# The biases of a graph network's products folded into a row of ones, and a maximum in place of a Relu

## The chip, the cores and the metric

The kernel runs on one core of a Trainium2 chip. The core has five engines that run their own instruction queues and wait for each other by semaphores: TensorE (PE, matrix products into PSUM), VectorE (DVE, element by element work), ScalarE (ACT, functions, copies, scale and bias), GpSimd (POOL, element by element work[...]) and SyncE (SP, which here only issues DMA transfers). The metric is device microseconds of one execution, from which the median of several runs is taken.

## The reference, cut to what matters

There are 64 graphs of 256 nodes with 256 channels. Layer 0 normalizes the adjacency matrix by its degrees, mixes the nodes with it, applies a linear map with bias `b0`, adds the residual and takes a layer norm. Its result is `x1`, so each node's channels of `x1` sum to zero. Layer 1 works on `x1`:

```
h      = relu(bn1(conv1 x1))                        # 1x1 convolution: a product over channels
x_conv = relu(bn2(conv2 h) + x1)                    # 17 taps along the nodes
s      = x1 w_se^T + b_se;  A = exp(-|s_n - s_m|^2) # 3 columns
x_nmp  = A relu(x1 w_msg^T + b_msg)
gi     = [x_conv, x_nmp] w_ih^T + b_ih;   gh = x1 w_hh^T + b_hh      # three blocks r, z, n
r, z   = sigmoid(gi_r + gh_r), sigmoid(gi_z + gh_z)
new    = (1 - z) tanh(gi_n + r gh_n) + z x1
out    = layernorm(x1 + new)
```

All of it is fp32.

## The kernel before, in words

The work goes graph by graph, in 4 groups of Q = 16 graphs. `layer0(g)` makes `x1`, stores it in `x1_d` and leaves it in SBUF. `x1_transposed(g)` transposes it on PE and copies it with ScalarE (L429) into `xn[:, :2]`, the channels on the partitions. `layer1(g)` then forms, in this order: `h` (conv1, with the three columns of `w_se` beside it, 259 columns; VectorE adds the bias row `bc1` for each half of the nodes, L446, and ScalarE takes the Relu of both halves, L447); the columns of `s` for the distances (L451 to L456, `scols`); `msg` (VectorE adds `bmsg_t`, L467, ScalarE takes the Relu, L468); the transform of `h` along the nodes (`p_dft`, L480); the distances and `A` (`p_rows`, `p_dist`, `aT`); and `x_nmp` (`p_nmp`, L513). The transposed `x1` and `x_nmp` go to DRAM as `xn_d[g]`.

conv2 is done for 16 graphs at once in a frequency domain: products with the transformed taps (`p_k`, L539), and the transform back, a long series of VectorE instructions on the tile `VM` (L588 to L747), which ends with stores to `xc_d`.

The gates of a graph are `gru(g)`. `load_gate` and `load_conv` fetch `x1`, `xn_d` and `xc_d`; `transposed(g)` brings x_conv into `inputs` (where `in_blocks` is true, for the first 4 graphs of each group and all 16 of the last, 28 in all, by a VectorE transpose in blocks, L805, an addition of the transposed `x1` on GpSimd, L806, and two Relus on ScalarE, L808; for the other 36 by PE transposes, L814, and two Relus, L816). `input_sums` forms four sums on GpSimd (L825 to L830). The r and z products use a Winograd form of seven block products of 128 by 256 with the weights `wrz`: 42 matrix instructions a graph (L846) into the four PSUM banks `p15`, `p26`, `p7`, `p34`. VectorE adds the bias `brz_t` while it moves `p15` out (`first`, L859), then forms the other sums (L860 to L869). The n products are 24 instructions (L883) into `p_n`, whose left half holds gi_n and right half gh_n, with `bn_t` added to both (L888), then L889, L892 and a tanh (L895), and the layer norm of the result (L906 to L910 with `layernorm`, L320 to L333). `p15`, `p26`, `p7`, `p34` and `p_n` share a pool of four banks (`psacc`), so the first `p_n` of a graph takes the bank of `p15` when L859 has read it.

Three things set the order of the instructions. Generators are advanced in a written order (`graphs`, `gates`, `merge`). In the stretches run by `paced`, each instruction passed to `mark` lets some pieces of the transform back be traced, and `tc.issue_after` queues those of its instructions that are on the marked instruction's engine behind it. And the compiler's list scheduler, which runs a model of the engines, fixes the order within each engine's queue: among the instructions that are ready in its model the earlier traced one goes first.

Of the kernel before, what the change touches and what calls it, by code (L numbers as in the profile page):

```python
# [9 lines left out]
F32 = mybir.dt.float32  # L10
# [4 lines left out]
P = 128  # L15
# [11 lines left out]
def kernel(  # L27
# [87 lines left out]
    wc1 = const.tile([P, DCH, D + NSE], F32)  # L115
    bc1 = const.tile([P, D + NSE], F32)
    wmsg = const.tile([P, DCH, D], F32)
    bmsg_t = const.tile([P, D], F32)
    alpha_t = const.tile([P, 1], F32)
# [6 lines left out]

    nc.scalar.copy(bc1[:, :4], neg_half)
    for i, a in enumerate((bn1_g, bn2_g, bn1_b, bn2_b, bn1_m, bn2_m, bn1_v, bn2_v)):
# [5 lines left out]
    nc.sync.dma_start(wc1[:, :, D:], w_seT.rearrange("(k p) o -> p k o", p=P))  # L134
    nc.sync.dma_start(bc1[:, D:], bcast_rows(b_se, NSE))


    ident = const.tile([P, P], F32)
    make_identity(nc, ident)
    nc.vector.tensor_scalar(alpha_t, alpha_t, MIN_ALPHA, None, op0=ALU.max)  # L140

# [11 lines left out]
    wn = const.tile([P, 3 * DCH, D], F32)  # L153
    brz_t = const.tile([P, 2, D], F32)
    bn_t = const.tile([P, 2, D], F32)

    bn2_bias = const.tile([P, DCH], F32)

    def batch_norms(pool):


        scale = pool.tile([P, D], F32, name="scale")
        p = bank("p_bn")
        nc.tensor.transpose(p[:, :16], vectors, ident[:16, :16])
        cols = pool.tile([P, 4, 4], F32, name="bn")
        nc.vector.tensor_copy(cols.rearrange("p i n -> p (i n)"), p[:, :16])
        g, b, m, v = (cols[:, i, :] for i in range(4))
        nc.vector.tensor_scalar(v, v, BN_EPS, None, op0=ALU.add)
        nc.gpsimd.tensor_tensor(v, v, neg_half, op=ALU.pow)
        nc.vector.tensor_mul(g, g, v)  # L170
        nc.vector.tensor_mul(m, m, g)
        nc.vector.tensor_sub(b, b, m)
        nc.vector.tensor_copy(bn2_bias, b[:, 2:4])

        ones = pool.tile([P, P], F32, name="ones")
        nc.vector.memset(ones, 1.0)
        rows = [bank("p_norm") for _ in range(2)]
        for i, col in enumerate((g[:, 0:1], g[:, 1:2], b[:, 0:1], b[:, 1:2], g[:, 2:3], g[:, 3:4])):
            diagonal = pool.tile([P, P], F32, name="diagonal", bufs=2)
            nc.vector.tensor_scalar(diagonal, ident, col, None, op0=ALU.mult)  # L180
            nc.tensor.matmul(rows[i // 4][:, i % 4 * P : (i % 4 + 1) * P], ones, diagonal, start=True, stop=True)
        nc.scalar.activation(scale, rows[1][:, :D], AF.Copy, scale=2.0 / FL)
        nc.vector.tensor_mul(
            wc1[:, :, :D], wc1[:, :, :D], rows[0][:, :D].unsqueeze(1).to_broadcast([P, DCH, D])
        )
        nc.vector.tensor_copy(bc1[:, :D], rows[0][:, D:])
        yield scale
# [234 lines left out]
    def x1_transposed(g):  # L422
        x1 = X1.pop(g)
        xn = XN[g] = work.tile([P, 2 * DCH, N], F32, name="xn")
        p = bank("p_x1T").rearrange("p (k n) -> p k n", k=DCH)
        for k in range(DCH):
            for c in range(NCH):
                nc.tensor.transpose(p[:, k, c * P : (c + 1) * P], x1[:, c, k * P : (k + 1) * P], ident)
        nc.scalar.copy(xn[:, :DCH], p)  # L429

    def layer1(g, place):
# [6 lines left out]

        h = work.tile([P, NCH, D + NSE], F32, name="h", bufs=1)
        for c in range(NCH):  # L440
            p = bank("p_conv1")[:, : D + NSE]
            for k in range(DCH):
                nc.tensor.matmul(  # L443
                    p, x1T[:, k, c * P : (c + 1) * P], wc1[:, k, :], start=k == 0, stop=k == DCH - 1
                )
            mark(nc.vector.tensor_tensor(h[:, c, :], p, bc1, op=ALU.add))  # L446
        nc.scalar.activation(h[:, :, :D], h[:, :, :D], AF.Relu)  # L447

        s3 = h[:, :, D:]
        cols = scols.rearrange("p c (q r) -> p c q r", r=32)  # L450
        nc.vector.tensor_copy(cols[:, :, :, :NSE], s3.unsqueeze(2).to_broadcast([P, NCH, 4, NSE]))  # L451
        sq3 = small.tile([P, NCH, NSE], F32, name="sq3")
# [9 lines left out]
        for c in range(NCH):  # L462
            for k in range(DCH):
                nc.tensor.matmul(  # L464
                    p[:, c, :], x1T[:, k, c * P : (c + 1) * P], wmsg[:, k, :], start=k == 0, stop=k == DCH - 1
                )
        mark(nc.vector.tensor_tensor(msg, p, bmsg_t.unsqueeze(1).to_broadcast([P, NCH, D]), op=ALU.add))  # L467
        nc.scalar.activation(msg, msg, AF.Relu)  # L468
        yield
# [288 lines left out]

    GATE, CONV, SUMS = {}, {}, {}

# [21 lines left out]
    def load_gate(g):  # L782
# [3 lines left out]
        nc.sync.dma_start(inputs[:, : 2 * DCH], xn_d[g])  # L786
        GATE[g] = x1, inputs

    def sent(g):
# [10 lines left out]
    def transposed(g):  # L800
# [3 lines left out]
        if in_blocks(g):  # L804
            behind(nc.vector.transpose(xcT.rearrange("p k (s r) -> p k s r", r=RB), CONV.pop(g)))  # L805
            nc.gpsimd.tensor_tensor(xcT, xcT, inputs[:, :DCH], op=ALU.add)  # L806
            for k in range(DCH):
                nc.scalar.activation(xcT[:, k], xcT[:, k], AF.Relu, bias=bn2_bias[:, k : k + 1])  # L808
            return
# [22 lines left out]
    def gru(g):  # L832
# [25 lines left out]
        first = gate.tile([P, 2, D], F32, name="first", tag="gn")  # L858
        mark(nc.vector.tensor_add(first, half(p15), brz_t), 1)  # L859
        nc.vector.tensor_add(trz[:, 0:2], first[:, 0:1].to_broadcast([P, 2, D]), half(p26))  # L860
# [13 lines left out]
        for c in range(NCH):  # L874
# [6 lines left out]
            for o, part in ((1, terms[:DCH]), (0, terms[DCH:])):  # L881
# [5 lines left out]
            gn = gate.tile([P, 2, D], F32, name="gn")  # L887
            mark(nc.vector.tensor_add(gn, p.rearrange("p (i d) -> p i d", i=2), bn_t), 1)  # L888
            nc.vector.scalar_tensor_tensor(  # L889
                gn[:, 1, :], trz[:, 2 * c], 1.0, gn[:, 1, :], op0=ALU.add, op1=ALU.mult  # L890
            )
# [81 lines left out]
    with tc.tile_pool(name="setup", bufs=1) as setup:  # L973
        load_taps(setup, 0)
        nc.sync.dma_start(wmsg, w_msgT.rearrange("(k p) o -> p k o", p=P))
        nc.sync.dma_start(bmsg_t, bcast_rows(b_msg, D))
        firsts = merge(layer0(0), layer0(1))
# [6 lines left out]
        def gate_weights():  # L984
# [8 lines left out]
            for k, w in ((0, w_hhT), (DCH, w_ihT[D:]), (2 * DCH, w_ihT[:D])):  # L993
                nc.sync.dma_start(wn[:, k : k + DCH], w[:, 2 * D :].rearrange("(k p) o -> p k o", p=P))
            yield

# [6 lines left out]
        others = [weights(setup, i, scale2) for i in range(NPARTS)]  # L1003
        others += [take(more_weights, i) for i in (1, 2, 2)]
        run(graphs(0, range(Q), others))
        bih_t = setup.tile([P, 3 * D], F32, name="bih", tag="taps", bufs=2)
        nc.sync.dma_start(bih_t, bcast_rows(b_ih, 3 * D))
        bhh_t = setup.tile([P, 3 * D], F32, name="bhh", tag="taps", bufs=2)
        nc.sync.dma_start(bhh_t, bcast_rows(b_hh, 3 * D))
        brz = brz_t.rearrange("p i d -> p (i d)")  # L1010
        nc.vector.tensor_add(brz, bih_t[:, : 2 * D], bhh_t[:, : 2 * D])
        nc.vector.tensor_sub(brz_t[:, 1], brz_t[:, 1], brz_t[:, 0])
        nc.vector.tensor_copy(bn_t[:, 0, :], bih_t[:, 2 * D :])
        nc.vector.tensor_copy(bn_t[:, 1, :], bhh_t[:, 2 * D :])
    ustream = ctx.enter_context(tc.tile_pool(name="ustream", bufs=6))
# [142 lines left out]
```

## Time and profile before

| | us |
|---|---|
| median of 3 runs | 2145.82 |
| lowest and highest run | 2143.14, 2146.74 |
| span of the profiled execution | 2152.3 |
| busy in it: PE, DVE, ACT, POOL | 2052.7, 1581.6, 841.9, 664.8 |

The profile is of one execution. Its span, from the first to the last instruction, is 2152.3 us, and what lies around the span is not shown, so that execution took at least 2152.3 us, which is 6.5 us (0.3%) above the median of the runs. A profile line such as `L888 DVE TENSOR_TENSOR gn<-p_n,bn_t 128x512 ... x128 | 87.3, 682 | 17.8` names the line of the code, the engine, the operation, output and inputs, the shape and the count, then the busy time in us and the mean duration of one in ns, then the idle time of the engine just ahead of these instructions, and what ended it.

### The profile page before, as it was taken

To read this page: it belongs to the slowest core of one execution; us is meant where nothing else is said; L and a number is where in the kernel's file an instruction comes from. 1 tells how busy PE (TensorE), PEld (TensorE's weight loads), DVE (VectorE), ACT (ScalarE), POOL (GpSimd) and SP (SyncE) were. 2 spreads that over 40 slices of the span, in tenths; PEclk is the share of its full clock that TensorE was granted. 3 is DMA by queue.
4 is the path that set the end of the run, shared out by engine and by line. 5 is a ranking of instruction groups with operands and counts; after the bars stand their busy time and mean duration, and the time that the engine had idled before them with its cause. 6 is when DMAs were issued, how large, how long until landed. Compare 5 with 4: busy or idle time off the path is not lost.

```text
span 2152.3 us, 28977 instructions
## 1 busy us (share of the span) xinstructions
PE 2052.7 (95%) x9693; PEld 1735.8 (81%) x9693; DVE 1581.6 (73%) x3719; ACT 841.9 (39%) x1857; POOL 664.8 (31%) x640
## 2 busy tenths in 40 slices
PE   7999999887999999899999999999999998999997
PEld 5888788776888888788888888777888887788886
DVE  5555578775568788775656988876566889988887
ACT  4665643456431123445552122446553112222222
POOL 2444310121431244213322133323231123444442
PEclk9999999999999999999999999999999999999999
DMA  4766666434346644233326654324324744443331
GB/s 122 235 196 197 198 194 207 142 132 134 96 146 203 203 110 128 93 112 113 113 94 190 205 157 113 118 98 133 102 88 136 243 116 122 119 102 99 94 84 54
DMA packets 295085, 298.30 MB, mean 139 GB/s; under 512 B 76414, under 2 KB 273618, under 8 KB 294938
## 3 DMA queue, kind: packets, MB, share of 16 engines
q1 hardware_dynamic: 235050, 200.46, 30.9%
q10 hardware_dynamic: 44480, 67.39, 8.8%
q0 software_dynamic: 15408, 28.61, 6.1%
q8 instruction: 77, 1.26, 0.2%
q14 instruction: 70, 0.57, 0.1%
HBM read 193.28 MB, written 103.06 MB: 138 GB/s over the span
## 4 chain that ended last, share of the span: by engine, by line
PE 44%; DVE 12%; issue 9%; POOL 6%; ACT 4%; DMA 2%; ACTq 0%; SPq 0%; POOLq 0%; DVEq 0%
PE p_rz L846 14%; PE p_n L883 8%; PE p_k L539 7%; PE p_out L409 2%; PE p_nmp L513 2%; PE p_hT L399 2%; PE p_dft L480 2%; POOL ln_rs L323 2%; PE p_conv L443 1%; PE p_msg L464 1%; PE p_dist L504 1%; POOL sums L826 1%; POOL sums L825 1%; DMA u<-ud 1%; POOL xc_g L796 1%
## 5 line engine op out<-in xcount | busy, mean ns | idle before, releaser
L883 PE MATMUL p_n<-wn,inputs 128*128 128x256 f32 x1536 | 355.1, 385 | 13.4 <-DVE first L859 13.2
L846 PE MATMUL p_rz<-wrz,sums 128*128 128x256 f32 x1536 | 348.6, 380 | 1.3 <-DVE gn L888 0.8
L883 PEld LDWEIGHTS p_n<-wn,inputs 128*128 128x128 f32 x1536 | 288.5, 192 | 64.2 <-DVE first L859 20.9
L846 PEld LDWEIGHTS p_rz<-wrz,sums 128*128 128x128 f32 x1536 | 290.0, 190 | 44.5 <-issue 5.2
L846 PE MATMUL p_rz<-wrz,inputs 128*128 128x256 f32 x1152 | 271.6, 379 | 1.0 <-ACT inputs L808 1.0
L323 POOL TENSOR_TENSOR ln_rs<-ln_rs,neg_half 128x2 f32<-128x2 f32 x129 | 99.1, 768 | 510.9 <-DVE ln_rs L322 464.0
L846 PEld LDWEIGHTS p_rz<-wrz,inputs 128*128 128x128 f32 x1152 | 217.6, 190 | 31.1 <-ACT inputs L808 1.2
L895 ACT ACTIVATE nn<-gn 128x256 f32<-128x256 f32 x128 | 53.3, 417 | 332.1 <-DVE gn L892 331.7
L539 PE MATMUL p_k<-u,VM 128*128 128x256 f32 x736 | 175.2, 380 | 2.7 <-DMA u<-ud 1.9
L369 POOL TENSOR_TENSOR dis<-deg,neg_half 128x2 f32<-128x2 f32 x64 | 46.1, 720 | 423.6 <-DVE deg L367 393.1
L333 ACT ACTIVATE x_g<-x_g,ln_mr,ln_rs 128x256 f32<-128x256 f32 x128 | 70.0, 593 | 241.5 <-DVE ln_mr L331 241.5
L539 PEld LDWEIGHTS p_k<-u,VM 128*128 128x128 f32 x736 | 138.1, 190 | 24.4 <-DMA u<-ud 4.1
L480 PE MATMUL p_dft<-fwd,h 128*128 128x240 f32 x512 | 120.2, 379 | 25.9 <-ACT h L447 24.6
L399 PE MATMUL p_hT<-adjT,x 128*128 128x256 f32 x512 | 129.8, 397 | 14.0 <-DVE adjT L381 7.6
L825 POOL TENSOR_TENSOR sums<-inputs 128x384 f32<-128x384 f32 x64 | 67.1, 1048 | 239.0 <-ACT inputs L816 206.3
L480 PEld LDWEIGHTS p_dft<-fwd,h 128*128 128x128 f32 x512 | 95.2, 192 | 47.6 <-ACT h L447 41.2
L506 DVE TENSOR_TENSOR aT<-aT,adjT 128x512 f32<-128x512 f32 x64 | 44.6, 698 | 118.2 <-ACT aT L505 118.1
L443 PE MATMUL p_conv<-wc,xn 128*128 128x259 f32 x512 | 125.8, 388 | 4.3 <-ACT xn L429 4.3
L392 POOL TENSOR_TENSOR x_t<-x_t,b_t 128x512 f32<-128x512 f32 x64 | 85.4, 1334 | 142.6 <-ACT x L391 97.4
L409 PE MATMUL p_out<-w,hT 128*128 128x256 f32 x512 | 123.1, 383 | 1.4 <-ACT hT L404 0.7
L464 PE MATMUL p_msg<-wmsg,xn 128*128 128x256 f32 x512 | 121.4, 380 | 0.0
L513 PE MATMUL p_nmp<-aT,msg 128*128 128x256 f32 x512 | 121.2, 379 | 0.2 <-DVE aT L506 0.2
(157 smaller groups left out, 3910.2 us busy)
## 6 DMA issues: line engine op xcount, KB each, us to landing
u<-ud SPq DMA_DIRECT2D x284, 256.0 KB
xn_d<-xn ACTq DMA_DIRECT2D x64, 512.0 KB
inputs<-xn_d SPq DMA_DIRECT2D x64, 512.0 KB
ud<-u_set POOLq DMA_DIRECT2D x39, 480.0 KB, 6.1
adj_t<-in_adj_dram SPq DMA_DIRECT2D x64, 256.0 KB
x_t<-in_x_dram SPq DMA_DIRECT2D x64, 256.0 KB
x_d<-x ACTq DMA_DIRECT2D x64, 256.0 KB
xc_d<-VM SPq DMA_DIRECT2D x64, 256.0 KB
```

The lines of the kernel that those rows point to most:

```text
L323: nc.gpsimd.tensor_tensor(rs[:, : len(chunks)], rs[:, : len(chunks)], neg_half[:, : len(chunks)], op=ALU.pow)
L392: nc.gpsimd.tensor_tensor(x_t, x_t, b0_t.unsqueeze(1).to_broadcast([P, NCH, D]), op=ALU.add)
L399: nc.tensor.matmul(p[:, k, :], x1[:, mc, k * P : (k + 1) * P], adjT[:, mc, 1 - mc : 3 - mc, :].rearrange("p n q -> p (n q)"), start=mc == ...
L409: nc.tensor.matmul(p[:, c, :], hT[:, k, c * P : (c + 1) * P], w0[:, k, :], start=k == 0, stop=k == DCH - 1)
L443: nc.tensor.matmul(p, x1T[:, k, c * P : (c + 1) * P], wc1[:, k, :], start=k == 0, stop=k == DCH - 1)
L464: nc.tensor.matmul(p[:, c, :], x1T[:, k, c * P : (c + 1) * P], wmsg[:, k, :], start=k == 0, stop=k == DCH - 1)
L480: nc.tensor.matmul(p[:, t0 * FL : t1 * FL], h[:, c, k * P : (k + 1) * P], fwd[:, first : first + t1 - t0, :].rearrange("p t f -> p (t f)") ...
L513: nc.tensor.matmul(p[:, k, :], msg[:, mc, k * P : (k + 1) * P], aT[:, mc].rearrange("p n q -> p (n q)"), start=mc == 0, stop=mc == NCH - 1,)
L539: nc.tensor.matmul(p[:, j * D : (j + 1) * D], v[:, k, :], u[:, k, :], start=k == 0, stop=k == DCH - 1)
L825: nc.gpsimd.tensor_tensor(S[:, 0], A21, A22, op=ALU.add)
L846: nc.tensor.matmul(p[:, j * D : (j + 1) * D], a[:, k], wrz[:, b, k], start=k == 0, stop=k == HALF - 1)
L883: nc.tensor.matmul(p[:, o * D : (o + 1) * D], lhsT, w, start=j == 0, stop=j == len(part) - 1)
```

## The change

The change replaces the first channel of the transposed `x1` by ones. Since a node's channels sum to zero, the first one is minus the sum of the others, so a product with weights W over all channels equals a product over the others with W less its first row; the first row of the weights is then free to hold the bias, which meets the row of ones.

- `xn[:, 0]` is written by an ACTIVATE with a per-partition scale (0 for the first channel, 1 for the others) and a per-partition bias (1 for the first), and `xn[:, 1]` by a copy: two ScalarE instructions for one.
- `wc1`, `wmsg`, `B11`, `T1` and `wn` lose their first row, which is loaded on all partitions (`top`, `hh_top`); the biases are put in its place. For `wc1` and `wmsg` the subtraction and the two small loads are GpSimd's, for the gate weights it is VectorE's work.
- `h` is a maximum with 0 on VectorE straight from PSUM; the columns of `s` are copied from PSUM for each half of the nodes.
- `msg` is a Relu on ScalarE straight from PSUM, and that is the marked instruction.
- `first` is a copy on ScalarE, and that is the marked instruction.
- `bn_t` is added to the left half of `p_n` alone; the next instruction reads the right half from PSUM.
- In the `in_blocks` graphs the first channel of `x1`, which the row of ones displaced, is loaded by itself (256 elements of 4 bytes), added on one partition by GpSimd, and the ones are taken off in the bias `bn2_less`.

```diff
--- before.py
+++ after.py
...
     wc1 = const.tile([P, DCH, D + NSE], F32)
-    bc1 = const.tile([P, D + NSE], F32)
     wmsg = const.tile([P, DCH, D], F32)
-    bmsg_t = const.tile([P, D], F32)
     alpha_t = const.tile([P, 1], F32)
...
-    nc.scalar.copy(bc1[:, :4], neg_half)
+    warm = const.tile([P, 4], F32)
+    nc.scalar.copy(warm, neg_half)
...
     nc.sync.dma_start(wc1[:, :, D:], w_seT.rearrange("(k p) o -> p k o", p=P))
-    nc.sync.dma_start(bc1[:, D:], bcast_rows(b_se, NSE))
 
...
+    unit, others_only = ident[:, 0:1], const.tile([P, 1], F32, name="others_only")
+    nc.vector.tensor_scalar(others_only, unit, -1.0, 1.0, op0=ALU.mult, op1=ALU.add)
+
+    def without_first(w, top, engine):
+        engine.tensor_tensor(w, w, top.unsqueeze(1).to_broadcast([P, DCH, top.shape[-1]]), op=ALU.subtract)
...
-    brz_t = const.tile([P, 2, D], F32)
-    bn_t = const.tile([P, 2, D], F32)
+    bn_t = const.tile([P, D], F32)
...
+    bn2_less = const.tile([P, 1], F32)
...
         nc.vector.tensor_copy(bn2_bias, b[:, 2:4])
+        nc.vector.tensor_sub(bn2_less, bn2_bias[:, 0:1], unit)
...
-        nc.vector.tensor_copy(bc1[:, :D], rows[0][:, D:])
+        nc.vector.tensor_copy(wc1[0:1, 0, :D], rows[0][0:1, D:])
...
@@ -426,7 +432,8 @@
         for k in range(DCH):
             for c in range(NCH):
                 nc.tensor.transpose(p[:, k, c * P : (c + 1) * P], x1[:, c, k * P : (k + 1) * P], ident)
-        nc.scalar.copy(xn[:, :DCH], p)
+        nc.scalar.activation(xn[:, 0], p[:, 0], AF.Identity, bias=unit, scale=others_only)
+        nc.scalar.copy(xn[:, 1], p[:, 1])
...
-        h = work.tile([P, NCH, D + NSE], F32, name="h", bufs=1)
+        h = work.tile([P, NCH, D], F32, name="h", bufs=1)
...
-            mark(nc.vector.tensor_tensor(h[:, c, :], p, bc1, op=ALU.add))
-        nc.scalar.activation(h[:, :, :D], h[:, :, :D], AF.Relu)
-
-        s3 = h[:, :, D:]
-        cols = scols.rearrange("p c (q r) -> p c q r", r=32)
-        nc.vector.tensor_copy(cols[:, :, :, :NSE], s3.unsqueeze(2).to_broadcast([P, NCH, 4, NSE]))
+            mark(nc.vector.tensor_scalar(h[:, c, :], p[:, :D], 0.0, None, op0=ALU.max))
+            nc.vector.tensor_copy(cols[:, c, :, :NSE], p[:, D:].unsqueeze(1).to_broadcast([P, 4, NSE]))
+
+        s3 = cols[:, :, 0, :NSE]
...
-        mark(nc.vector.tensor_tensor(msg, p, bmsg_t.unsqueeze(1).to_broadcast([P, NCH, D]), op=ALU.add))
-        nc.scalar.activation(msg, msg, AF.Relu)
+        mark(nc.scalar.activation(msg, p, AF.Relu))
...
+        if in_blocks(g):
+            FIRST[g] = gate.tile([1, N], F32, name="x1_first")
+            with nc.allow_non_contiguous_dma("one channel"):
+                nc.sync.dma_start(FIRST[g], x1_d[g // Q][g % Q][:, 0:1].rearrange("n d -> d n"))
...
             behind(nc.vector.transpose(xcT.rearrange("p k (s r) -> p k s r", r=RB), CONV.pop(g)))
             nc.gpsimd.tensor_tensor(xcT, xcT, inputs[:, :DCH], op=ALU.add)
-            for k in range(DCH):
-                nc.scalar.activation(xcT[:, k], xcT[:, k], AF.Relu, bias=bn2_bias[:, k : k + 1])
+            nc.gpsimd.tensor_tensor(xcT[0:1, 0], xcT[0:1, 0], FIRST.pop(g), op=ALU.add)
+            for k in (1, 0):
+                nc.scalar.activation(xcT[:, k], xcT[:, k], AF.Relu, bias=bn2_bias[:, 1:2] if k else bn2_less)
             return
...
         first = gate.tile([P, 2, D], F32, name="first", tag="gn")
-        mark(nc.vector.tensor_add(first, half(p15), brz_t), 1)
+        mark(nc.scalar.copy(first, half(p15)), 1)
         nc.vector.tensor_add(trz[:, 0:2], first[:, 0:1].to_broadcast([P, 2, D]), half(p26))
...
             gn = gate.tile([P, 2, D], F32, name="gn")
-            mark(nc.vector.tensor_add(gn, p.rearrange("p (i d) -> p i d", i=2), bn_t), 1)
+            mark(nc.vector.tensor_add(gn[:, 0, :], p[:, :D], bn_t), 1)
             nc.vector.scalar_tensor_tensor(
-                gn[:, 1, :], trz[:, 2 * c], 1.0, gn[:, 1, :], op0=ALU.add, op1=ALU.mult
+                gn[:, 1, :], trz[:, 2 * c], 1.0, p[:, D:], op0=ALU.add, op1=ALU.mult
             )
...
     with tc.tile_pool(name="setup", bufs=1) as setup:
         load_taps(setup, 0)
         nc.sync.dma_start(wmsg, w_msgT.rearrange("(k p) o -> p k o", p=P))
-        nc.sync.dma_start(bmsg_t, bcast_rows(b_msg, D))
+        top = setup.tile([P, 2 * D + NSE], F32, name="top")
+        nc.sync.dma_start(top[:, :D], bcast_rows(conv1T, D))
+        nc.sync.dma_start(top[:, D : D + NSE], bcast_rows(w_seT, NSE))
+        nc.sync.dma_start(top[:, D + NSE :], bcast_rows(w_msgT, D))
+        without_first(wc1, top[:, : D + NSE], nc.gpsimd)
+        without_first(wmsg, top[:, D + NSE :], nc.gpsimd)
+        nc.gpsimd.dma_start(wc1[0:1, 0, D:], b_se.rearrange("(a d) -> a d", a=1))
+        nc.gpsimd.dma_start(wmsg[0:1, 0], b_msg.rearrange("(a d) -> a d", a=1))
...
+            top = setup.tile([P, 3, D], F32, name="hh_top", tag="taps", bufs=2)
+            nc.sync.dma_start(top.rearrange("p i d -> p (i d)"), bcast_rows(w_hhT, 3 * D))
+            rows = setup.tile([1, 2, 3, D], F32, name="gate_bias", tag="taps", bufs=2)
+            for i, v in enumerate((b_hh, b_ih)):
+                nc.sync.dma_start(rows[:, i].rearrange("p i d -> p (i d)"), v.rearrange("(a d) -> a d", a=1))
+            nc.sync.dma_start(bn_t, bcast_rows(b_ih[2 * D :], D))
+            yield
+
+            for i, w in enumerate((wrz[:, B11], wrz[:, T1], wn)):
+                with tc.issue_after(marks[-1][0]):
+                    without_first(w[:, :DCH], top[:, i], nc.vector)
+                    if i < 2:
+                        nc.vector.tensor_add(w[0:1, 0], rows[:, 0, i], rows[:, 1, i])
+                    else:
+                        nc.vector.tensor_copy(w[0:1, 0], rows[:, 0, i])
             yield
...
-        others += [take(more_weights, i) for i in (1, 2, 2)]
+        others += [take(more_weights, i) for i in (1, 3, 2)]
         run(graphs(0, range(Q), others))
-        bih_t = setup.tile([P, 3 * D], F32, name="bih", tag="taps", bufs=2)
-        nc.sync.dma_start(bih_t, bcast_rows(b_ih, 3 * D))
-        bhh_t = setup.tile([P, 3 * D], F32, name="bhh", tag="taps", bufs=2)
-        nc.sync.dma_start(bhh_t, bcast_rows(b_hh, 3 * D))
-        brz = brz_t.rearrange("p i d -> p (i d)")
-        nc.vector.tensor_add(brz, bih_t[:, : 2 * D], bhh_t[:, : 2 * D])
-        nc.vector.tensor_sub(brz_t[:, 1], brz_t[:, 1], brz_t[:, 0])
-        nc.vector.tensor_copy(bn_t[:, 0, :], bih_t[:, 2 * D :])
-        nc.vector.tensor_copy(bn_t[:, 1, :], bhh_t[:, 2 * D :])
```

More of the change, by code (lines that the diff above doesn't have):

```diff
@@ L437, in layer1 @@
         yield
-        h = work.tile([P, NCH, D + NSE], F32, name="h", bufs=1)
+        h = work.tile([P, NCH, D], F32, name="h", bufs=1)
+        cols = scols.rearrange("p c (q r) -> p c q r", r=32)
         for c in range(NCH):
@@ L756, in complex_end @@
             yield from output(q, n + 12, im + 3, re + 3)
-    GATE, CONV, SUMS = {}, {}, {}
+    GATE, CONV, SUMS, FIRST = {}, {}, {}, {}
     EARLY = 4
```

## The prediction

> **What bounds the kernel now.** I read the page's busy times first, then PE's waits, then PE's idle time by stage, then the order of instructions inside the two worst stages.
>
> ```profile
> PE 2052.7 (95%) x9693; PEld 1735.8 (81%) x9693; DVE 1581.6 (73%) x3719; ACT 841.9 (39%) x1857; POOL 664.8 (31%) x640
> ```
>
> The change removes no matrix instruction, so PE's 2052.7 us are a floor, and all there is to win is the 99.6 us of the span in which PE is idle. Who ends that idle time is in the waits of PE:
>
> ```profile
> PE p_dft L480 <- ACT h L447: 24.6, 18, 8.0
> PE p_n L883 <- DVE first L859: 13.2, 11, 2.4
> PE p_hT L399 <- DVE adjT L381: 7.6, 7, 2.1
> ...
> PE p_conv L443 <- ACT xn L429: 4.3, 6, 0.7
> PE p_hT L399 <- DVE msg L467: 3.8, 4, 1.0
> ```
>
> Columns: total us, times, longest. Three of the rows (h, first, msg: 41.6 us) wait for instructions that the change rewrites. The stages, from a table of busy time by window (length, PE busy, DVE busy, ACT busy):
>
> ```profile
> 0.00:42.00 42.00, 27.76 (x102) 21.82 (x103) 22.70 (x153) 16.12 (x38) 9.69 (x19) 0.88 0.37 112
> ...
> 400.00:520.00 120.00, 104.67 (x499) 82.98 (x497) 91.28 (x289) 68.59 (x158) 25.85 (x26) 0.99 0.38 126
> 520.00:640.00 120.00, 110.49 (x516) 93.58 (x516) 66.51 (x165) 54.18 (x117) 45.13 (x42) 0.97 0.41 115
> ...
> 1745.00:1905.00 160.00, 148.66 (x685) 127.62 (x683) 150.86 (x312) 36.23 (x77) 65.22 (x57) 0.99 0.44 118
> 1905.00:2130.00 225.00, 224.87 (x1030) 194.63 (x1031) 188.36 (x328) 64.85 (x127) 100.65 (x95) 1.00 0.32 89
> ```
>
> In most stages PE is full. From 1745 to 1905 VectorE is the bound (151 of 160 us: the gates of one group beside the transform back of the next), and PE idles 11.3 us. From 760 to 920 and 1270 to 1430 VectorE is at 133 and 134 of 160 and PE idles 9.0 each.
>
> **What the Trainium skill says.** "SBUF — State Buffer", section "Who interferes with whom": a VectorE instruction with two SBUF inputs contends with a GpSimd instruction that reads SBUF, one with at most one SBUF input doesn't. The trace agrees: L889 (both inputs SBUF) takes 424 ns in the median and up to 1495, L888 (one from PSUM) 675 to 693 always. "ScalarE: Activation LUTs", section "What ACT_TABLE_LOAD costs": each per-partition scale or bias adds about 93 ns. The trace: a 256-column copy from PSUM takes 362 (L580), one with a bias 468 (L816); with a scale, SBUF, 507 (L391) against 417 without (L895).
>
> **The change part by part.** Back-to-back VectorE instructions overlap by some 0.08 us in the timeline, so a removed one frees its duration less 0.08.
>
> *VectorE.* In the rows below, L859 goes and L888 halves.
>
> ```profile
> L888 DVE TENSOR_TENSOR gn<-p_n,bn_t 128x512 f32<-128x512 f32 x128 | 87.3, 682 | 17.8 <-PE p_n L883 17.4
> L889 DVE SCALAR_TENSOR_TENSOR gn<-trz,gn 128x256 f32<-128x256 f32 x128 | 69.9, 546 | 1.6
> L467 DVE TENSOR_TENSOR msg<-p_msg,bmsg_t 128x512 f32<-128x512 f32 x64 | 43.7, 683 | 20.5 <-PE p_msg L464 20.5
> L865 DVE TENSOR_TENSOR trz<-trz,p_rz 128x256 f32<-128x256 f32 x64 | 26.5, 413 | 1.9 <-PE p_rz L846 0.7
> L859 DVE TENSOR_TENSOR first<-p_rz,brz_t 128x512 f32<-128x512 f32 x64 | 42.9, 670 | 5.8 <-PE p_rz L846 5.5
> ```
>
> Per graph of gates: L859 670 - 80 = 590; L888 twice 682 - 413 (L865, the same shape) = 538; L889 twice 546 - 477 (L414, the nearest with one PSUM input) = 138, bounded by 0 and 2 x (546 - 413). Together 1.27 us. Per graph of layer 1: L467, 0.60 us. L446 (421) becomes a maximum from PSUM over 256 columns, 413 to 426 (L865, L497): nothing. The `s` copy (294) becomes two of 12 columns at about 142 each (L166): nothing.
>
> *ScalarE.* L447 (630) goes; L468 (628) becomes 585 from PSUM (L404); L429 (586) becomes 362 + 107 + 90 = 559 and 362, less 0.09 overlap: +245; `first` adds 585. Layer 1 loses 0.43 us a graph, the gates gain 0.59. At 39% busy this lies beside PE, except where an instruction is queued behind another's wait; then it costs that wait. For PE the split of L429 is worth nothing: the first half is ready 0.03 us earlier, the second 0.24 later, when PE has a product of 0.24 us to do.
>
> *GpSimd.* 28 additions on one partition, about 0.73 us (from L825 at 384 columns, 1000, and L806 at 512, 1270). In the last stage `transposed` ends at 2119.5, but the next sums start at 2122.86, behind L323: 3.4 us cover the 0.7; without them it would be 28 x 0.7 = 20. SP's 28 small loads go out behind `inputs`, as long as the 0.47 us of the other short-row load (L134); they land before L806 has ended. They delay only later loads on SP by 0.5, against a graph of 14.5.
>
> *Start.* SP loses two broadcasts (bmsg_t, b_se) and issues three; POOL gets two subtractions of 1.3 us and two DMA issues of 0.57 (L310). The `b0` broadcast of the same size was waited for until 10.9, 4.7 us after its issue at 6.2, so the last `top` lands near 18.5, and POOL's 3.8 us fall on 17.5 to 22, beside idle time from 16.1 to 20.6. L323 at 20.6 and L169 at 23.4 stand behind. I take 1 us lost, between 0 and 4. The gate weights' six VectorE instructions (three of 0.68, three of 0.41) replace four (1.19, 0.80, 0.41, 0.26) near 243 us, where PE is full from other work: nothing, at most the 0.6 us between them; their loads wait for the same `taps` buffers as `bih` and `bhh` did and move 518 KB in place of 768.
>
> *On the path*, stage by stage:
> - 1745 to 1905: VectorE bound, 9 graphs x 1.27 = 11.4, but PE's idle 11.3 caps it. I take 9.
> - 760 to 920 and 1270 to 1430: each has h 2.0, msg 1.9 and first 1.4 us of PE waits. Without L447, h is 0.63 plus a semaphore, about 0.7, earlier: 1.4 of its 2.0. With msg and first: 4.7 each, 9.4.
> - 400 to 520: four h waits, 2.8 at 0.7 each; L381 queues behind L467 on VectorE, so 0.6 of each of six waits: 3. Together 5.8.
> - 520 to 640: 8.0 us of PE waiting for L447 behind eleven copies of L1052 on ScalarE. p_dft can go, and the next PE work (p_rows, 0.4) too; then p_hT waits for L379, behind the same copies. 1.9 + 0.4 = 2.3, plus 0.5 for a second h wait: 2.8.
> - 920 to 1150, 1430 to 1650: six h waits at 0.7: 4.1.
> - 1905 to 2130: a graph takes 14.47 us for 66 products of 0.216, 14.24. The 0.23 is the start of p_n behind L859, which VectorE reaches after the layer norm's statistics. I take 0.17 x 15 = 2.5.
> - End: L888 halved on the last chain, 0.3.
>
> The sum is 33.9 - 1 = 32.9. Against it I set what the profile can't show: msg and first now wait in ScalarE's queue. They are ready beside 57 to 60% of busy time from 42 to 520, and the order of all queues is made anew. I take 9 off, bounded by -5 and 30. Net 24 us: the profiled execution would go from 2152.3 to 2128, the median, 6.5 lower, from 2145.8 to 2122.
>
> **Rivals.**
> - *The waits only move* (p_n then waits for the copy in ScalarE's queue, p_dft for the maximum in VectorE's). For it: in the stages with the waits VectorE is busy for 76 to 84% and ScalarE up to 57%, so a wait of 0.7 us is easily made again by one instruction ahead. Against it: VectorE waits 11.7 us for p_conv before L446, so it is mostly there in time. Then only VectorE's stage gains, 2145.8 - 9 + 5 = 2142, the same within 0.2%.
> - *Slower: first stands behind the layer norm on ScalarE.* In program order the two L333 of graph g precede the copy for g + 1.
>
> ```profile
> 1790.32 0.65 DVE L859 TENSOR_TENSOR first<-p_rz,brz_t 128x512 f32<-128x512 f32 x1
> ...
> 1791.02 5.45 PE L883 MATMUL p_n<-wn,inputs 128*128 128x256 f32 x24 [2.44 <-DVE first L859]
> ...
> 1792.18 1.09 ACT L333 ACTIVATE x_g<-x_g,ln_mr,ln_rs 128x256 f32<-128x256 f32 x2 [5.23 <-DVE ln_mr L331]
> ```
>
> If the scheduler puts it there, p_n starts after 1793.3 + 0.6 + 0.1 = 1794.0 in place of 1791.0: 3.0 x 9 = 27 lost and the 9 not won: 2145.8 - 15 + 27 = 2158. It decides where the model has L331 done before p15 is; in both stages that I looked at, VectorE took L859 before L322, so `first` was ready sooner. Near 798 us it took L859 after L331.
> - *Marks without effect*: a piece of the transform behind a mark on ScalarE isn't held back on VectorE, and one comes between L888 and L889, so a bank of p_n is kept 0.4 to 1.2 us longer. In VectorE's stage alone, 9 x 1.2 = 11: 2133.
>
> **How the numbers follow.** A run of this kernel can be told from no change at about 0.2%, 4.3 us. Chances: forecast 0.55 (2106 to 2136), marks 0.15, waits move 0.13, first late 0.10, start and order worse than bounded 0.07 (2150). Faster by more than 0.2%: 0.55 + 0.15 and a third of the third, 0.75; same 0.07; slower 0.18. The range, 2104 to 2148, leaves out the late first and a tenth below.
>
> **What would show it.** Right: the wait of p_dft for h under 12 us in total and for VectorE; p_n's wait for first near 2, now for ScalarE; L889 with a maximum below 600 ns; DVE busy near 1460, ACT near 850; the stage of the last gates at 14.3 us a graph. Wrong: p_n waiting 2 us or more per graph for a copy behind L333; PE's idle time above 95 us; PE starting p_conv later than 34 us.

## The result, and the profile after

The kernel after takes 2156.20 us (median of 8 runs, 2151.38 to 2163.23) against 2145.74 us of the kernel before (8 runs): a ratio of 1.0048, 95% interval 1.0035 to 1.0060. I had forecast 2122, with a range that ended at 2148. Its profiled execution took 2151.38 us, span 2149.6: the fastest of its eight. That of the kernel before, with a span of 2152.3, was slower than all its eight runs, so the two traces side by side hide the loss.

The busy times of the kernel after:

```profile
PE 2042.5 (95%) x9693; PEld 1739.8 (81%) x9693; DVE 1445.3 (67%) x3659; ACT 861.5 (40%) x1921; POOL 694.7 (32%) x672
```

VectorE lost 136 us of work, as the change promised, and PE is idle for 107.1 us of the span (2149.6 - 2042.5) in place of 99.6. PE's waits in the kernel after (total us, times, longest), and last the one row of the kernel before that the comparison needs:

```profile
PE p_conv L451 <- ACT xn L436: 24.4, 19, 2.3
PE p_rows L498 <- DVE scols L462: 14.5, 11, 2.1
...
PE p_rows L498 <- ACT adjT L385: 6.5, 1, 6.5
...
PE p_rz L856 <- DVE gn L899: 4.1, 4, 1.5
...
PE p_dft L485 <- DVE scols L455: 1.2, 3, 0.7
...
PE p_rows L493 <- DVE scols L456: 3.7, 4, 1.3
```

The waits that were to go are gone: 24.6 us of `p_dft` for `h` became 1.2 for the columns of `s`, and 13.2 of `p_n` for `first` became nothing. A new wait is as long as the largest that went: `p_conv` waits 24.4 us for L436, the second half of the copy of `x1T`, which the change split in two. The wait of `p_rows` for the columns of `s` was 3.7 us and is 14.5.

By stage (window, length, busy time and count of PE, PEld, which is PE's loading of weights, DVE, ACT and POOL, then granted clock, share of the DMA engines and GB/s), first the kernel after:

```profile
42.00:285.00 243.00, 223.87 (x1079) 183.62 (x1078) 115.63 (x325) 136.71 (x319) 102.68 (x93) 0.99 0.60 189
400.00:520.00 120.00, 106.60 (x504) 85.68 (x503) 89.70 (x274) 59.93 (x146) 22.26 (x21) 0.96 0.39 125
...
760.00:920.00 160.00, 155.99 (x755) 134.91 (x754) 127.15 (x304) 60.58 (x133) 56.00 (x53) 1.00 0.42 122
...
920.00:1270.00 350.00, 338.72 (x1622) 288.25 (x1621) 220.68 (x568) 146.51 (x333) 95.35 (x96) 1.00 0.46 138
...
1745.00:1905.00 160.00, 155.91 (x737) 135.63 (x736) 146.55 (x317) 42.47 (x89) 64.79 (x57) 1.00 0.46 126
1905.00:2130.00 225.00, 225.00 (x1044) 198.37 (x1044) 146.07 (x323) 73.16 (x144) 118.88 (x112) 1.00 0.35 89
```

and three of the same windows in the kernel before:

```profile
42.00:285.00 243.00, 237.26 (x1161) 195.03 (x1160) 135.59 (x360) 146.56 (x343) 103.10 (x99) 1.00 0.62 196
...
760.00:920.00 160.00, 150.98 (x710) 127.65 (x709) 133.22 (x308) 57.71 (x129) 54.24 (x51) 0.98 0.37 107
...
920.00:1270.00 350.00, 345.79 (x1658) 294.22 (x1658) 242.65 (x579) 144.33 (x320) 93.60 (x92) 1.00 0.48 145
```

Compare the counts of matrix instructions. From 1745 to 1905 PE did 737 in place of 685, from 760 to 920 755 in place of 710: the gains came where they were forecast. From 42 to 285 it did 1079 in place of 1161. At 0.216 us each, those 82 are 17.7 us lost, in a stage of which the prediction said nothing but that ScalarE is busy there. A further 36 are lost from 920 to 1270.

One graph of that stage in the timeline of the kernel after (start, duration, engine):

```profile
239.57 0.57 ACT L435 ACTIVATE xn<-p_x1T,ident,others_only 128x256 f32<-128x256 f32 x1
...
241.06 1.04 PE L451 MATMUL p_conv<-wc,xn 128*128 128x259 f32 x4
...
242.33 0.16 DVE L337 SCALAR_TENSOR_TENSOR ln_mr<-ln_mv,ln_rs 128x2 f32<-128x2 f32 x1 [1.78 <-POOL ln_rs L329]
...
242.52 1.09 ACT L339 ACTIVATE x<-x,ln_mr,ln_rs 128x256 f32<-128x256 f32 x2 [2.38 <-DVE ln_mr L337]
243.52 0.35 ACT L436 COPY xn<-p_x1T 128x256 f32<-128x256 f32 x1
...
243.92 1.14 PE L451 MATMUL p_conv<-wc,xn 128*128 128x259 f32 x4 [0.96 <-ACT xn L436]
```

The two halves of the copy do not stand together. In ScalarE's queue the layer norm of another graph (L339, two instructions) is between them, and it waits 2.38 us for VectorE, which waits for GpSimd's L329. L436 needs nothing of all that: its input was complete at 239.5. But this queue ran in order, so L436 runs at 243.52 instead of about 240.1. PE does the four products that need only the first half, then what else is ready (`p_adjT`, two of `p_u`), then waits 0.96 us. With one copy there was nowhere to put the layer norm but before or after the whole. In ScalarE's queue of the kernel after, a layer norm of `x` stands between the halves in 39 of the 64 graphs.

### The profile page after: what moved, and what is told of

The parts are those of the page before. It is cut to its first block, busy times and chain, and to the rows that moved or that the text cites. A ratio compares the mean times of both kernels' runs of the same rounds, so it can differ in the third digit from the quotient of the medians.

```text
span 2149.6 us, 29255 instructions
## 1 busy us (share of the span) xinstructions
PE 2042.5 (95%) x9693; PEld 1739.8 (81%) x9693; DVE 1445.3 (67%) x3659; ACT 861.5 (40%) x1921; POOL 694.7 (32%) x672
## 4 chain that ended last, share of the span: by engine, by line
PE 55%; DVE 7%; issue 5%; POOL 4%; ACT 3%; DMA 1%; ACTq 0%; POOLq 0%; DVEq 0%; SPq 0%
PE p_rz L856 21%; PE p_n L893 12%; PE p_k L544 8%; PE p_hT L405 2%; PE p_out L415 2%; PE p_nmp L518 2%; PE p_conv L451 2%; PE p_msg L470 2%; PE p_dft L485 2%; POOL ln_rs L329 1%; PE p_dist L509 1%; POOL xc_g L805 1%; POOL sums L836 1%; POOL sums L840 1%; DMA u<-ud 0%
## 5 line engine op out<-in xcount | busy, mean ns | idle before, releaser
L893 PE MATMUL p_n<-wn,inputs 128*128 128x256 f32 x1536 | 348.7, 381 | 0.0
L329 POOL TENSOR_TENSOR ln_rs<-ln_rs,neg_half 128x2 f32<-128x2 f32 x129 | 99.9, 774 | 433.5 <-DVE ln_rs L328 372.9
L451 PE MATMUL p_conv<-wc,xn 128*128 128x259 f32 x512 | 132.3, 392 | 28.8 <-ACT xn L436 24.4
L451 PEld LDWEIGHTS p_conv<-wc,xn 128*128 128x128 f32 x512 | 94.1, 191 | 53.4 <-ACT xn L436 33.6
L339 ACT ACTIVATE x_g<-x_g,ln_mr,ln_rs 128x256 f32<-128x256 f32 x128 | 70.0, 593 | 148.4 <-DVE ln_mr L337 148.4
L405 PEld LDWEIGHTS p_hT<-adjT,x 128*128 128x128 f32 x512 | 96.7, 199 | 29.1 <-ACT dist_l L500 6.7
```

The lines of the kernel that those rows point to most:

```text
L329: nc.gpsimd.tensor_tensor(rs[:, : len(chunks)], rs[:, : len(chunks)], neg_half[:, : len(chunks)], op=ALU.pow)
L339: nc.scalar.activation(y[:, c, :], y[:, c, :], AF.Identity, bias=mr[:, c : c + 1], scale=rs[:, c : c + 1])
L405: nc.tensor.matmul(p[:, k, :], x1[:, mc, k * P : (k + 1) * P], adjT[:, mc, 1 - mc : 3 - mc, :].rearrange("p n q -> p (n q)"), start=mc == ...
L451: nc.tensor.matmul(p, x1T[:, k, c * P : (c + 1) * P], wc1[:, k, :], start=k == 0, stop=k == DCH - 1)
L893: nc.tensor.matmul(p[:, o * D : (o + 1) * D], lhsT, w, start=j == 0, stop=j == len(part) - 1)
```

## The experiments

**Theory: the torn pair.** The loss is L436, the second half of the pair, behind the layer norm. Without it the kernel after would take 2128 to 2138 us, 10 to 20 less than the kernel before. **Rivals:** the split by itself, 0.25 us of ScalarE a graph; the start; the wait for `s`; or the gains aren't there. Each run stands beside the kernel before on the same chip (medians 2147 to 2150); ratios are given with their 95% intervals.

### The split alone

```diff
-        nc.scalar.copy(xn[:, :DCH], p)
+        nc.scalar.copy(xn[:, 0], p[:, 0])
+        nc.scalar.copy(xn[:, 1], p[:, 1])
```

> The kernel before, with the copy of x1T split into its two halves and nothing else changed. Theory (torn pair): the scheduler puts the two layer norm instructions of the next graph, which wait 2.4 us for GpSimd and VectorE, between the halves, as it did in the kernel after, so p_conv waits about 1 us more for the second half in some 20 to 30 graphs: 15 to 28 us slower than the kernel before, 2161 to 2174, and a wait of p_conv for the second half of 15 us or more. Rival (the split costs ScalarE 0.25 us a graph and nothing else, and the loss of the kernel after lies elsewhere): within 4 us of the kernel before.

Measured: 2166.83 us against 2147.95, ratio 1.0093 (1.0078 to 1.0108), 20 us lost. In the waits of PE of this kernel:

```profile
PE p_dft L481 <- ACT h L448: 23.6, 18, 8.0
PE p_conv L444 <- ACT xn L430: 23.0, 18, 2.4
```

The second line is new, the first is as before. The split alone loses 20 us, of the size of the whole gain that I had forecast (24). ScalarE's own work hardly grew: it is busy for 846.0 us in place of 841.9, so the 0.25 us a graph of the rival was itself too high. The loss has its place in the first stage:

```profile
42.00:285.00 243.00, 223.00 (x1083) 183.15 (x1081) 126.36 (x332) 138.99 (x335) 102.42 (x93) 0.99 0.60 190
```

These are 78 products fewer than in the kernel before, nearly the 82 of the kernel after.

### One copy, and an earlier transposition

In the kernel after, the pair mended in two ways: one copy (which leaves no row of ones), or the whole change with the transposition of the next graph written ahead of `p_nmp`. The control puts that into the kernel before.

```diff
# one_copy
-        nc.scalar.activation(xn[:, 0], p[:, 0], AF.Identity, bias=unit, scale=others_only)
-        nc.scalar.copy(xn[:, 1], p[:, 1])
+        nc.scalar.copy(xn[:, :DCH], p)
# early_transpose, early_before: layer1 calls x1_transposed(g + 1) where g is in ALONE
-    ALONE = set()
+    ALONE = set(range(B - 1))
```

> The kernel after with one copy of both halves of x1T, so the row of ones isn't made. Theory (torn pair): the 24.4 us that PE waits for the second half go, and with them a little of the lost clock: 2128 to 2138. Rival (the loss comes from the start, from s or from the new order of the queues): 2150 to 2158. If the gates and layer 1 bring nothing either and only the pair matters, it ends at the time of the kernel before, 2143 to 2149.

> The kernel after, whole, with the transposition of the next graph's x1 written ahead of the product p_nmp (as it already is in one stage), so that both halves of the copy stand ahead of the layer norm in the order of the text and next to each other in ScalarE's queue. Theory (torn pair): as with one copy, 2128 to 2138, and a wait of p_conv for the second half under 5 us; the split by itself costs nothing. Rival (0.25 us of ScalarE a graph is itself on the path): 5 us or more above the kernel with one copy. Rival (the loss lies elsewhere): 2150 to 2158.

> The kernel before with the same earlier transposition, as a control. Theory (torn pair): it has no pair to tear and p_conv waits only 4.3 us for the copy, so it stays within 5 us of the kernel before, 2141 to 2149. Rival (the earlier transposition is a gain by itself, whatever the pair): it gains 15 us or more, to 2131 or less.

Measured: one copy 2112.91 (0.9839, 0.9824 to 0.9854), early transposition 2112.53 (0.9830, 0.9817 to 0.9843), the control 2159.27 (1.0051, 1.0037 to 1.0066). Both remedies give the same time, within their intervals. One of them keeps the second instruction and the other does not, so no cost of that instruction by itself can be seen; the earlier transposition also moves other work, so a small cost could hide. Both gain more than the theory asked for, 35 to 37 us on the kernel before in place of 10 to 20. The earlier transposition is no gain of its own: in the kernel before it loses 11 us, where I had expected 5 at most. There `p_dft` waits longer for `h` (39.0 us in place of 24.6).

So tearing the pair costs 20 us in the kernel before and, by the two remedies, 45 to 47 us in the changed one. The first stage holds about the same loss in both; what lies behind the rest, in the later stages, no run takes apart.

The pair in the timeline of the kernel with the early transposition:

```profile
227.87 0.56 ACT L435 ACTIVATE xn<-p_x1T,ident,others_only 128x256 f32<-128x256 f32 x1 [1.08 <-PE p_x1T L434]
...
228.34 0.36 ACT L436 COPY xn<-p_x1T 128x256 f32<-128x256 f32 x1
...
231.13 1.92 PE L451 MATMUL p_conv<-wc,xn 128*128 128x259 f32 x8
...
233.72 1.09 ACT L339 ACTIVATE x<-x,ln_mr,ln_rs 128x256 f32<-128x256 f32 x2 [3.54 <-DVE ln_mr L337]
```

L436 starts before L435 has ended, `p_conv` runs as one group of eight with no wait, and the layer norm comes after. This is the version to keep: the whole change, and 1.7% faster than the kernel before.

### The parts by themselves

The gates' part and layer 1's part put into the kernel before, one at a time and together, with no row of ones. The biases that these parts would need are left out.

```diff
# gates_alone
-        mark(nc.vector.tensor_add(first, half(p15), brz_t), 1)
+        mark(nc.scalar.copy(first, half(p15)), 1)
...
-            mark(nc.vector.tensor_add(gn, p.rearrange("p (i d) -> p i d", i=2), bn_t), 1)
+            mark(nc.vector.tensor_add(gn[:, 0, :], p[:, :D], bn_t[:, 0, :]), 1)
...
-                gn[:, 1, :], trz[:, 2 * c], 1.0, gn[:, 1, :], op0=ALU.add, op1=ALU.mult
+                gn[:, 1, :], trz[:, 2 * c], 1.0, p[:, D:], op0=ALU.add, op1=ALU.mult
# layer1_alone
...
-            mark(nc.vector.tensor_tensor(h[:, c, :], p, bc1, op=ALU.add))
-        nc.scalar.activation(h[:, :, :D], h[:, :, :D], AF.Relu)
+            mark(nc.vector.tensor_scalar(h[:, c, :], p[:, :D], 0.0, None, op0=ALU.max))
+            nc.vector.tensor_copy(cols[:, c, :, :NSE], p[:, D:].unsqueeze(1).to_broadcast([P, 4, NSE]))
...
-        mark(nc.vector.tensor_tensor(msg, p, bmsg_t.unsqueeze(1).to_broadcast([P, NCH, D]), op=ALU.add))
-        nc.scalar.activation(msg, msg, AF.Relu)
+        mark(nc.scalar.activation(msg, p, AF.Relu))
```

> The kernel before with the gates' part of the change alone: first is copied by ScalarE, the sum for gn takes 256 columns and the product reads PSUM; their biases (zero in this data) are left out, and nothing of layer 1, the split or the start is changed. Theory (the prediction's sum holds part by part): 9 from VectorE's stage, 2.8 from the waits for first in the two stages before, 2.5 in the last gates, 0.3 at the end: 14.6 us faster, 2133 (2129 to 2137). Rival (the waits only move): 6 us faster or less, 2142 or more. Rival (all of the gain over 33 us sits here, since VectorE is the engine relieved): 2120 or less.

> The kernel before with layer 1's part alone: h by a maximum on VectorE, s copied straight from PSUM, msg by one Relu on ScalarE; their biases (zero in this data) are left out. Theory (part by part): h and msg in the two stages before the gates 6.6, 5.8 in 400 to 520, 2.8 in 520 to 640, 4.1 in the two later ones: 19.3 us faster, 2129 (2124 to 2134). Rival (the wait for h only moves on to p_rows, which waits for s behind it): 8 us faster or less, 2140 or more.

> The kernel before with both parts, without their biases: no row of ones, no split, nothing at the start, no first channel in the gates. Theory: the sum of the two parts, 34 us, so 2114, and 2 to 4 us below the kernel after with one copy of x1T, which also has the start (2.3 us by PE's timeline) and 28 additions on GpSimd: 2108 to 2113. Rival (what is left of the row of ones costs 8 us or more): 2105 or less. Rival (the two parts win the same waits, VectorE's): above 2120.

Measured: gates 2127.38 (0.9901, 0.9883 to 0.9919), 21 us gained (17 to 25); layer 1 2127.70 (0.9898, 0.9881 to 0.9916), 22 us gained (18 to 26); both 2107.47 (0.9803, 0.9784 to 0.9823), 42 us gained (38 to 46). The two add up, as they would if they win different waits. Layer 1 is within its forecast; the gates gained 21 where the sum had 14.6, and both together end 0.5 us under the forecast of 2108 to 2113.

### What is left of the row of ones

The kernel after with the early transposition, and: no subtractions from layer 1's weights at the start, with their loads and bias rows left out too; those subtractions on VectorE; no loads and additions of the first channel in the gates; `s` copied ahead of the maximum.

```diff
# no_start: without these, the three loads of top ahead and the two of biases behind
...
-        without_first(wc1, top[:, : D + NSE], nc.gpsimd)
-        without_first(wmsg, top[:, D + NSE :], nc.gpsimd)
...
# start_on_vector: the same two with nc.vector
# no_first: without this and its load
-            nc.gpsimd.tensor_tensor(xcT[0:1, 0], xcT[0:1, 0], FIRST.pop(g), op=ALU.add)
# early_s_first: the two instructions exchanged
+            nc.vector.tensor_copy(cols[:, c, :, :NSE], p[:, D:].unsqueeze(1).to_broadcast([P, 4, NSE]))
             mark(nc.vector.tensor_scalar(h[:, c, :], p[:, :D], 0.0, None, op0=ALU.max))
```

> The kernel after with the earlier transposition, without the subtractions from the weights of layer 1: no loads of top, no subtractions and no small DMA issues on GpSimd at the start, so these weights keep their first row. Theory (GpSimd's subtraction of wc runs beside three small VectorE instructions, which take 1.0 and 1.0 us longer): p_norm starts at 25.7 and p_conv near 31 as in the kernel before, 2.3 us sooner than in the kernel after, and nothing else moves: 2109 to 2112. Rival (the start delays loads as well and the loss grows in the first stage): 2107 or less.

> The kernel after with the earlier transposition and the two subtractions at the start on VectorE instead of GpSimd; they come to stand behind the first two instructions for the diagonal, while VectorE waits for p_norm. Theory (the small instructions were slowed by GpSimd's subtraction beside them): p_norm starts at 25.7 to 26.3 in place of 28.0, the second pair for the diagonal stands behind 1.3 us of subtractions, and p_conv starts at 31.5 to 32.3 in place of 33.1: the total falls by about 1 us, which is within its spread. Rival (something else, such as SyncE's later issues, holds the start): p_norm at 27.5 or later.

> The kernel after with the earlier transposition, without the 28 loads of the first channel of x1 and the 28 additions of it on GpSimd in the gates, so the first channel of the convolution's sum lacks x1. Theory (they are hidden): 2110 to 2114, as with them. Rival (the additions delay the next sums, in the gates at the end most): 0.4 us or more a graph in 28 graphs, 2101 or less.

> The kernel after with the earlier transposition and with the copy of s ahead of the maximum in each chunk. p_rows waits 6.1 us in total for s in the kernel with the earlier transposition alone. Theory (p_rows waits for the chain of small instructions behind the maximum): the chain starts up to 0.4 us sooner and p_dft gets h 0.16 later, so 1 to 4 us faster, 2108 to 2112. Rival (the chain is late because other VectorE work and GpSimd stand in its way): no change, 2111 to 2115.

Measured: 2112.25 (0.9839, 0.9825 to 0.9852), 2114.78 (0.9844, 0.9830 to 0.9857), 2108.92 (0.9820, 0.9807 to 0.9834) and 2114.50 (0.9835, 0.9813 to 0.9858), in the order of the list, against 0.9830 with none of them. No one of the four can be told from it.

- *The start.* Without it `p_norm` starts at 25.41 in place of 27.77 and `p_conv` at 30.46 in place of 32.89, but `p_msg` at 34.62 in place of 35.15: the first `p_conv` takes 3.82 us when it starts early and 1.99 when it starts late, so 0.5 of the 2.4 us is left after it. With the subtractions on VectorE `p_norm` starts at 25.51 and `p_conv` at 31.22, both a little ahead of what the theory said: GpSimd's subtraction was what held `p_norm`.
- *s first.* `p_rows` waits 3.0 us for `s` in place of 6.1, and `p_dft` has a new wait of 4.2 for `h`. Here the rival is right that a wait only moves, though by another way than it said.
- *The first channel.* 0.9820 against 0.9830, about 2 us, with overlapping intervals. The distance from both parts without the row of ones (0.9803) to the whole change mended (0.9830) is 6 us, again with overlapping intervals. What share of it is the additions' stays open.

## Why the prediction was wrong

**The step that failed** is the one on ScalarE: "For PE the split of L429 is worth nothing: the first half is ready 0.03 us earlier, the second 0.24 later, when PE has a product of 0.24 us to do." That takes the second half to follow the first at once. In 39 graphs it followed behind the layer norm, in the one shown 3.4 us later than it could. PE waited 24.4 us for it, and the group that waited is busy for 8.1 us more (`p_conv` 132.3 us; 124.2 with the early transposition). The prediction did say that an instruction queued behind another's wait costs that wait, but it applied this to `msg` and `first` alone. The allowance of "9 off, bounded by -5 and 30" for queues made anew was meant for such things. It was mis-sized: from the ratios 1.0048 and 0.9830 the torn pair cost about 47 us (45 by one copy). The two traces show 36.1 of it (2149.6 - 2113.5), since the one of the kernel after is its fastest run and the other the slowest of its five.

**A rival was near.** The second rival put `first` behind the layer norm in ScalarE's queue, at 3 us a graph, and ended at 2158. The mechanism came true with another instruction: `p_n` never waits for `first`. That the time came near is luck, since its 27 us were to fall on the gates, and the gates gained. The question that I asked of `first`, what can the scheduler put ahead of it, I did not ask of the second half.

**Point by point.**
- *VectorE.* Forecast near 1460 us of busy time, 1445.3 measured. L899 (L889 before) was to take 477 ns and takes 408, and its longest is 421, not 1495: with one input in PSUM it is free of GpSimd, as the Trainium skill's "SBUF — State Buffer", section "Who interferes with whom", has it.
- *ScalarE.* Forecast near 850, 861.5 measured; L435 567 ns (559), L436 357 (362), `first` 573 (585), `msg` 594 (585). The durations were right; the place was not.
- *The sum, without the queue.* 32.9 us forecast; 35 to 37 measured once the pair is mended. That is in part luck, because errors of the terms offset each other. By counts of products with the early transposition, the stages from 400 to 640 gained 14 (505 and 524 against 499 and 516), 3.0 us, where 8.6 was forecast, and those of 760 to 920 and 1270 to 1430 gained 70 (750 and 749 against 710 and 719), 15.1 us, where 9.4 was forecast. VectorE's stage was taken at 9 and gained 52 products in the kernel after, 11.2 us. In the last gates `p_n` starts every 14.41 us before and every 14.245 after: 0.166 x 15 = 2.5 us, as forecast.
- *The floor.* "PE's 2052.7 us are a floor" is false. With both parts PE is busy for 2033.1 us with the same 9693 instructions, at a granted clock of 0.992 in place of 0.990, which explains about 4 of the 20. Much of the rest shows in the groups that used to wait. Before, from the groups by line (busy us, mean ns, idle before):

```profile
L883 PE MATMUL p_n<-wn,inputs 128*128 128x256 f32 x1536 | 355.1, 385 | 13.4 <-DVE first L859 13.2
...
L480 PE MATMUL p_dft<-fwd,h 128*128 128x240 f32 x512 | 120.2, 379 | 25.9 <-ACT h L447 24.6
```

and after:

```profile
L893 PE MATMUL p_n<-wn,inputs 128*128 128x256 f32 x1536 | 348.7, 381 | 0.0
L451 PE MATMUL p_conv<-wc,xn 128*128 128x259 f32 x512 | 132.3, 392 | 28.8 <-ACT xn L436 24.4 <-ACT xn L435 3.5 <-issue 0.7
...
L485 PE MATMUL p_dft<-fwd,h 128*128 128x240 f32 x512 | 115.0, 367 | 1.3 <-DVE scols L455 1.2
```

`p_n` lost 13.2 us of waits and 6.4 of busy time, `p_dft` 5.2 of busy time beside its waits; with both parts alone they are down by 6.4 and 5.1. These two groups are shorter where they no longer wait, so gains were under-counted, and PE's idle time was no cap on them. What makes a group shorter isn't shown.
- *The waits only move.* In part: against the 23.4 us that `p_dft` no longer waits, `p_rows` has 10.8 more for the columns of `s` (14.5 against 3.7). With the early transposition it has 6.1 in all, so the greater part came with the torn pair. It also has one new wait of 6.5 us for L385, which stands behind the eleven copies on ScalarE that had held up `h` for 8.0 us. That the wait would move to this instruction was forecast, with `p_hT` and not `p_rows` as the one that waits; mending the pair does not remove it (6.3 of the 7.2 us that `p_rows` then waits for L385 are this one).
- *The start*, 1 us between 0 and 4: `p_conv` starts 2.4 us later, and nothing of it can be measured in the total. The subtractions were to fall on 17.5 to 22. They fell on 25.35, beside two small VectorE instructions on the path:

```profile
25.35 1.19 POOL L144 TENSOR_TENSOR wc<-wc,top 128x518 f32<-128x518 f32 x1
25.41 1.14 DVE L337 SCALAR_TENSOR_TENSOR ln_mr<-ln_mv,ln_rs 128x2 f32<-128x2 f32 x1 [0.50 <-POOL ln_rs L329]
...
26.55 1.30 DVE L186 TENSOR_SCALAR diagonal<-ident,bn 128x128 f32<-128x128 f32 x1
```

In the kernel before, the same two take 0.16 us and 0.28 at this place. A VectorE instruction of two elements a partition lasted as long as GpSimd's of 518 beside it. L337 has two SBUF inputs, but L186 has one and a scalar for each partition, so the rule as the prediction put it, that one SBUF input is safe, does not cover it. The same section of "SBUF — State Buffer" in the Trainium skill makes an exception for VectorE's two-port modes and counts `tensor_scalar` among the operations that can enter them; no run here shows which mode L186 was in.
- *The marks on ScalarE.* No large loss of theirs: in 121 of 128 cases nothing stands between L898 and L899, and the gates alone gained more than forecast. But PE waits 4.1 us, in four places of VectorE's stage, for L899, which is now the last reader of a bank of `p_n`; for L888 it waited 0.8. How much of this is the marks' isn't separated.
- *The signs.* All that were named for a right prediction came (h under 12 and for VectorE, `first` under 2, L889 under 600 ns, 14.3 us a graph), and one of those for a wrong one: PE idle above 95 us. Those for a right prediction tested the parts that were right.

## What to carry to other kernels

Splitting an instruction on an in-order queue is not free because its halves are short: ask what can be scheduled between them, what that waits for, and look for the pair in the timeline. Where the order follows the text, write the pair ahead of what could come between. Here a wait cost more than its row among the waits, for the group behind it was longer too. So count finished matrix instructions by window, not busy time, and move one suspect alone (here two lines) before you judge a change by its total.

## What the runs showed that I had not expected

PE's clock fell after some waits that are short. In the kernel after, PE's timeline at 70 us and at 293, and the windows around them:

```profile
69.61 1.04 PE L451 MATMUL p_conv<-wc,xn 128*128 128x259 f32 x4
...
73.46 2.01 PE L451 MATMUL p_conv<-wc,xn 128*128 128x259 f32 x4 [1.94 <-ACT xn L436]
75.26 2.75 PE L470 MATMUL p_msg<-wmsg,xn 128*128 128x256 f32 x8
...
293.02 1.14 PE L451 MATMUL p_conv<-wc,xn 128*128 128x259 f32 x4 [2.34 <-ACT xn L436]
294.00 1.89 PE L470 MATMUL p_msg<-wmsg,xn 128*128 128x256 f32 x8
...
70.00:80.00 10.00, 8.06 (x33) 6.51 (x33) 2.95 (x10) 5.11 (x11) 3.64 (x5) 0.83 1.00 297
290.00:300.00 10.00, 7.66 (x40) 6.08 (x38) 4.84 (x16) 5.05 (x11) 2.81 (x3) 1.00 0.29 100
```

After a wait of 1.94 us the same four products take 2.01 us in place of 1.04, and `p_msg` 2.75 in place of 1.89: 1.8 us more, nearly the wait again. The window from 70 to 80 has a granted clock of 0.83. At 243.92, after 0.96 us, the four take 1.14 and the clock stays. At 293.02, after 2.34 us, it stays as well, so the length of the last wait alone does not decide it. The Trainium skill's "TensorE: Matmul & The Clock Gate", section "What's actually happening", puts the fall after an idle window of some 3.4 us, one that runs freely; here a fall came with a wait of 1.94 us. The mean granted clock differs between runs of one kernel: those of the kernel after had 0.990 (2151 us) to 0.986 (2163 us), and the mended one 0.993 to 0.994. From the mean clocks of the two traces, 0.990 and 0.993, an estimate is that some 6 of their 36 us are the clock's (0.003 of about 2130); no run separates its share of the 47.
